# Loads of one image cut in eight parts, and a copy within DRAM cut in sixteen

## Chip, core and metric

The kernel runs on one core of a Trainium2 chip. The metric is the device time of one execution in microseconds (us), the median of three runs.

## What is computed

The input x has 4 images of 32 channels and 128 x 128 pixels. Layer 0 folds each 2 x 2 square of pixels into channels: 128 channels, 64 x 64 positions (cut from the reference):

```
xs = x.reshape(B, C, h, R, w, R).transpose(0, 1, 3, 5, 2, 4).reshape(B, C * R * R, h, w)
q = xs.reshape(B, C * R * R, hw)
energy = jnp.einsum('bci,bcj->bij', q, q)
d = jnp.sqrt(jnp.diagonal(energy, axis1=1, axis2=2))
attn = jax.nn.softmax(energy / (d[:, :, None] * d[:, None, :]), axis=-1)
out = gamma * jnp.einsum('bcj,bij->bci', q, attn) + xs      # and unfolded again
```

`energy` is 4096 x 4096 for each image, and symmetric. Layer 1 takes the result as tokens of 128 numbers, 4096 to an image: a linear attention with residual, then a mixture of eight experts of which each token uses two, with residual again.

## The kernel before

**Layer 0.** `attend` works on an image's 4096 positions in 8 chunks of 512. It goes through rows i = 0 to 7, and in row i through blocks (i, jc) with jc up to i, four steps to a block; step (i, t) is step t of row i, t = 4 jc + j. A step makes a 128 x 512 piece of the energy on TensorE (line 556, tile `pe`), its exponential on ScalarE (line 559, tile `pr`, "ACT" in the profile), and two steps later the product of it with q (line 440, tile `po`). Since the energy is symmetric, a block off the diagonal serves the other side too, transposed: VectorE (DVE) transposes pieces of 32 x 32 (line 369, tile `F`), and the rest of the transposition goes through DRAM. `move` writes `F` to a DRAM tile `blocks` (line 483), planned two steps after the block's last piece. `bring`, planned three steps later, reads it as tile `G` in four DMAs (line 491), and five steps later `transposed_share` starts to multiply it (line 375, tile `pg`), one quarter to a step. The diagonal blocks do the same with `below` (lines 498 and 506). So a block write has eight steps from its plan to its product, and a G load five. A full step has three pairs of products and takes 2.58 us.

**The loads of T.** Layer 1 needs the image's pixels again, by tokens. `input_rows` loads them into `T`, 32 rows of tokens in a partition, by `load_tokens` (line 279), which issues four DMAs on SP's queue for each call: four calls of eight rows, 128 KB to a DMA. The next image's first pixels are loaded by `prep` through the same function into `xx`.

**The copy within DRAM.** The experts' tokens are sorted through two DRAM tiles `xs`. Some of their places are never written, so `setup_sorting` fills both beforehand with any finite numbers: it copies pixels of x into them, eight DMAs of 624 KB on ACT's queue (line 154). The first scatter into `xs` starts at 514.9 us.

**The order.** PE, DVE, ACT and SP each run their instructions in the order in which the program issues them[...]. A table `timed` says when the side work goes in between the steps of image 0. An entry (generator, begin, end, count) lets the generator advance about `count` times between `begin` and `end` per cent of the image's clock; the clock goes up by 8 in a full step, by 4 more where a share goes along, and 1568 are an image. Two advances are made for each count, so a generator with two bare `yield`s after an item uses one count for it.

[...]

Of the kernel before, what the change touches and what calls it, by code (L numbers as in the profile page):

```python
# [22 lines left out]
def kernel(  # L23
# [43 lines left out]
    nc = tc.nc  # L67
    P = 128
    B, C, H, W = x.shape
# [6 lines left out]
    KT = 32  # L76
# [42 lines left out]
    NT = 2 * HR + E - 1  # L119
# [6 lines left out]
    xs = [dram.tile([NT * P, D], F32, tag=f"xs{h}", name=f"xs_{h}", bufs=1) for h in range(2)]  # L126
    xs_made, xs_read = ([], []), ([], [])
# [8 lines left out]
    def setup_sorting():  # L136
        def iota(dst, pattern, part=0):
            nc.gpsimd.iota(
                dst, pattern=pattern, base=0, channel_multiplier=part, allow_small_or_imprecise_dtypes=True
            )  # L140

        iota(rank_below, [[1, P]], part=-1)
        nc.vector.tensor_scalar(rank_below, rank_below, 0.0, None, ALU.is_gt)
        iota(upto, [[1, E], [-1, E]])
        nc.vector.tensor_scalar(upto, upto, 0.0, None, ALU.is_ge)
        iota(tiles_of[:, 0, :], [[P, HR]])
        iota(tile_no[:, :, 0], [[1, NT]])
        yield
        yield

        rows = x.rearrange("b c h w -> (b c h) w")
        step = NT * P // 4
        for g in range(8):
            inst = nc.scalar.dma_start(xs[g // 4][ts(g % 4, step), :], rows[ts(g, step), :])
            xs_made[g // 4].append(inst.ins)
            yield
            yield

# [19 lines left out]
    def idle(n):  # L178
        for _ in range(2 * n):
            yield  # L180
# [90 lines left out]
    def tokens(ap, b):  # L271
        return ap[b].rearrange("c (s k r) w -> s r c k w", s=2, r=2)

    def load_tokens(dst, b, k0, nk, queues=(nc.sync, nc.sync)):
        src = tokens(x, b)
        for s in range(2):
            for r1 in range(2):
                p0 = s * 64 + r1 * 32
                queues[r1].dma_start(dst[p0 : p0 + 32], src[s, r1, :, k0 : k0 + nk, :])
# [302 lines left out]
    def finish():  # L582

        while queued or late:
            yield
            tick[0] += 1
            turn_tick()
            clock[0] += 3 * NJ
            step_share()
            yield  # L590


    def input_rows(b, st):
        st["T"] = T = big1.tile([P, KT, D], F32, tag="T", name=f"T_{b}")
        for kc in range(4):
            load_tokens(T[:, ts(kc, 8), :], b, 8 * kc, 8)
            yield
            yield
            yield from idle(1)
# [703 lines left out]
    states = [{} for _ in range(B)]  # L1303
# [14 lines left out]
    timed = [(first, 0, 1, 4)]  # L1318
    for b in range(B):

        if b == 0:
            for kc, begin, end in ((1, 0, 5), (2, 6, 20), (3, 25, 45)):
                timed.append((prep(0, kc, states[0]), begin, end, 12))
            timed.append((setup_weights(), 46, 58, 9))
            timed.append((setup_sorting(), 58, 98, 9))
        if b + 1 < B:
            nxt = states[b + 1]
            timed.append((prep(b + 1, 0, nxt), 65, 82, 13))
            timed.append((prep(b + 1, 1, nxt), 83, 99, 13))
        timed.append((input_rows(b, states[b]), *((55, 75) if b in (0, B - 1) else (82, 99)), 9))  # L1330
        done = [0] * len(timed)
        start = clock[0]
        closing = None
        for half, _ in enumerate(chain(attend(b, states[b]), finish() if b == B - 1 else ())):
            if half % 2 == 0:
                t = 100 * (clock[0] - start) / UNITS
                moved = []
                if closing is None and t > 84:
                    closing = layer1(b, states[b])
                    steady.append([closing.first_parts() if b == B - 1 else closing.all_parts(), clock[0]])  # L1340
                for n, (steps, begin, end, count) in enumerate(timed):
                    if t >= begin and done[n] * (end - begin) < (t - begin) * count:
                        moved.append(steps)
                        done[n] += 1
                for stream in steady:
                    if clock[0] >= stream[1]:
                        stream[1] = clock[0] + PACE
                        moved.append(stream[0])
            for steps in moved:
                next(steps, None)  # L1350
        for steps, *_ in timed:
            for _ in steps:
                pass
        timed = []
        if b + 1 < B:
            timed.append((prep(b + 1, 2, nxt), 2, 20, 13))
            timed.append((prep(b + 1, 3, nxt), 30, 50, 13))
# [43 lines left out]
```

## Time and profile before

| | |
|---|---|
| median of three runs | 1744.91 us (1744.48 to 1747.42) |
| the profiled execution: its time, its span | 1753.19 us, 1751.4 us |
| mean granted TensorE clock | 0.983 |
| DMA, mean over the span | 204 GB/s |
| row 6 of image 0, from its first product to that of the diagonal | 207.65 to 281.92 us |
| T loads of image 0 on SP | from 213.45, 222.45, 251.01 and 267.03 us, four DMAs each |
| copies into `xs` on ACT | at 240.20, 255.72, 279.94, 295.24, 311.81, 325.99, 342.38, 358.55 us |

The profile is of one execution. A group names the line, the engine and the tiles (written <- read), the number of instructions, busy time and the mean of one, and then the time for which its engine stood idle just before them and what ended most of that. "SPq" and "ACTq" are DMA issues on those engines' queues. A wait is put down to the event that came last before it ended. In the order of time, a line has the start, the duration, the engine, the line of code and the tiles; brackets give the idle time before it and its releaser.

### The profile page before, as it was taken

What the parts mean: (1) busy time and instruction counts of PE and PEld (TensorE: products, weight loads), DVE (VectorE), ACT (ScalarE), POOL (GpSimd) and SP (SyncE); (2) the same over time, 40 slices, a digit from 0 to 9 for tenths busy, and PEclk for the clock granted to TensorE, in tenths of its full rate; (3) what the DMA queues carried; (4) which work ended last, traced back from release to release, by engine and by line L of the source; (5) the groups of instructions that cost most, each with busy time, mean ns of one, the idle gap of its engine ahead of it and who ended that gap; (6) DMA issues with size and microseconds to landing.
All of it is one profiled execution on the core that took longest, in us unless ns stands there. A gap on an engine that the chain in (4) does not pass through costs nothing. (4 is left out here: it accounts for less than half of the span.)

```text
span 1751.4 us, 21197 instructions
## 1 busy us (share of the span) xinstructions
PE 1667.8 (95%) x5458; PEld 882.2 (50%) x5458; DVE 939.7 (54%) x2443; ACT 927.0 (53%) x2893; POOL 512.0 (29%) x553
## 2 busy tenths in 40 slices
PE   8999998999999999899999999979999999899887
PEld 5444444455554455445554455535555455444633
DVE  4433333467485335566477334546748533455687
ACT  3555444466565555446565455536556455445376
POOL 1000000011026505540015622552102660463166
PEclk9999999999999999999999999989999999999989
DMA  4675877776568799997567799998656889995001
GB/s 136 195 207 166 217 200 222 237 212 190 165 195 239 232 276 252 264 243 197 164 189 223 227 273 264 251 244 224 192 166 196 251 223 271 265 267 133 1 13 37
DMA packets 240168, 355.24 MB, mean 203 GB/s; under 512 B 26928, under 2 KB 154928, under 8 KB 226096
## 3 DMA queue, kind: packets, MB, share of 16 engines
q1 hardware_dynamic: 219792, 314.91, 64.0%
q0 software_dynamic: 12288, 25.19, 5.1%
q10 hardware_dynamic: 7968, 13.77, 2.7%
q8 instruction: 46, 0.75, 0.2%
q14 instruction: 74, 0.61, 0.1%
HBM read 183.64 MB, written 173.15 MB: 204 GB/s over the span
## 5 line engine op out<-in xcount | busy, mean ns | idle before, releaser
L559 ACT ACTIVATE pr<-pe 128x512 f32<-128x512 f32 (+1 forms) x576 | 322.3, 560 | 546.3 <-PE pe L556 427.9
L440 PE MATMUL po<-pr,qT 128*128 128x512 f32 (+3 forms) x1152 | 553.2, 562 | 3.9 <-ACT o L445 3.5
L375 PE MATMUL pg<-G,qT 128*128 128x512 f32 x880 | 456.8, 601 | 37.5 <-DMA G<-blocks 25.6
L556 PE MATMUL pe<-qn,qn 128*128 128x512 f32 x896 | 464.7, 601 | 1.9 <-ACT pr L559 1.6
L369 DVE STREAM_TRANSPOSE F<-pr 128x512 f32<-128x512 f32 x440 | 305.9, 702 | 169.6 <-ACT pr L559 152.2
L440 PEld LDWEIGHTS po<-pr,qT 128*128 128x128 f32 x1152 | 217.1, 192 | 252.6 <-issue 224.8
L380 ACT ACTIVATE junk<-G 128x512 bf16<-128x512 f32 x440 | 273.1, 621 | 33.9 <-DMA G<-blocks 27.3
L375 PEld LDWEIGHTS pg<-G,qT 128*128 128x128 f32 x880 | 167.3, 192 | 239.6 <-issue 205.8
L1113 POOL DMA_INDIRECT yb<-ys,place x192 | 185.1, 964 | 275.6 <-DMA xn<-xs 103.2
L988 POOL DMA_INDIRECT xs<-xn,place x192 | 185.6, 967 | 125.5 <-issue 51.6
L556 PEld LDWEIGHTS pe<-qn,qn 128*128 128x128 f32 x896 | 156.0, 193 | 113.9 <-issue 103.5
L385 DVE TENSOR_TENSOR o<-o,pg 128x512 f32<-128x512 f32 x110 | 75.4, 685 | 201.4 <-PE pg L375 170.1
L164 POOL TENSOR_TENSOR rn<-ss,neg_half 128x8 f32<-128x8 f32 (+1 forms) x17 | 27.8, 1634 | 401.6 <-DVE ss L325 401.6
L559 ACT ACTIVATION_READ_ACCUMULATOR pr<-pe 128x1 f32 x576 | 112.1, 195 | 0.0
L1022 ACT ACTIVATE xn<-pys 128x256 f32<-128x256 f32 (+1 forms) x120 | 44.9, 376 | 116.1 <-PE pys L1055 69.3
L1048 PEld LDWEIGHTS pys<-ew_sb,xn 128*128 128x128 f32 x468 | 67.9, 191 | 57.2 <-issue 45.3
L164 POOL TENSOR_TENSOR rsf<-dm_f,neg_half 128x8 f32<-128x8 f32 (+1 forms) x15 | 26.2, 1746 | 235.1 <-DVE sv_f L635 235.1
L556 PE MATMUL pe<-qn 128*128 128x512 f32 (+3 forms) x256 | 90.2, 435 | 0.7 <-ACT qn L344 0.7
L380 ACT ACTIVATION_READ_ACCUMULATOR junk<-G 128x1 f32 x440 | 84.4, 192 | 0.0
L1048 PE MATMUL pys<-ew_sb,xn 128*128 x468 | 71.8, 276 | 11.4 <-ACT xn L1022 5.4
L1031 DVE COPY result<-pys 128x256 f32<-128x256 f32 (+1 forms) x60 | 24.6, 410 | 101.6 <-ACT xn L1022 46.2
L164 POOL TENSOR_TENSOR rsa<-dm_a,neg_half 128x8 f32<-128x8 f32 x16 | 26.4, 1647 | 167.4 <-DVE sv_a L635 167.1
(189 smaller groups left out, 1618.5 us busy)
## 6 DMA issues: line engine op xcount, KB each, us to landing
blocks<-F SPq DMA_DIRECT2D x108, 1024.0 KB
G<-blocks SPq DMA_DIRECT2D x432, 256.0 KB
xn<-xs SPq DMA_DIRECT2D x114, 128.0 KB
below<-F SPq DMA_DIRECT2D x31, 384.0 KB
G<-below SPq DMA_DIRECT2D x124, 96.0 KB
T<-in_x_dram SPq DMA_DIRECT2D x64, 128.0 KB
out_dram<-acc SPq DMA_DIRECT2D x128, 64.0 KB
xx<-in_x_dram SPq DMA_DIRECT2D x62, 128.0 KB
```

The costliest lines, as they stand in the source:

```text
L164: pinned(nc.gpsimd.tensor_tensor(dst, src, neg_half.to_broadcast(list(src.shape)), ALU.pow))
L369: f()
L375: nc.tensor.matmul(pg.rearrange("p (a f) -> p a f", a=4), st["qT"][i][:, ib, :], G[:, :, ib], start=(ib == 0), stop=(ib == NJ - 1),)
L380: nc.scalar.activation(junk, G[:, :, ib], AF.Copy, accum_out=st["sums"][:, NJ * i + ib, jc : jc + 1])
L385: nc.vector.tensor_tensor(o, o, pg.rearrange("p (a j c) -> p a j c", a=4, c=S), ALU.add)
L440: nc.tensor.matmul(row["po"][:, lo:hi], qT[blk // NJ][:, blk % NJ, :], w, start=start, stop=(row["left"] == 0))
L556: nc.tensor.matmul(pe[:, c0:], qn[jc][:, ts(j, P)], qn[i][:, c0:], start=True, stop=True)
L559: nc.scalar.activation(pr[:, c0:], pe[:, c0:], AF.Exp, accum_out=sums[:, t, i : i + 1]).ins
L988: inst = nc.gpsimd.indirect_dma_start(xs[h], offset(place[:, i, k : k + 1]), xn[:, k, :], None)
L1022: nc.scalar.activation(bufs[4 + g % 2][:, :n], p[:, : n * P].rearrange("p (j t) -> p j t", t=P), AF.Copy)
L1048: nc.tensor.matmul(p[:, 2 * P + j * D : 2 * P + j * D + D], bufs[4 + g % 2][:, j, :], weights[:, bass.ds(begins[2 * (g % 2) + j], D)], sta ...
L1113: inst = nc.gpsimd.indirect_dma_start(yb[k // 4][:, i, k % 4, :], None, ys, offset(place[:, i, k : k + 1]))
```

## The change

The copy into `xs` is made in sixteen DMAs of 312 KB in place of eight of 624 KB, with two `yield`s behind each as before. Image 0's T is loaded in eight calls of four rows (64 KB to a DMA) in place of four calls of eight; the other images keep four. In the table, the setup of the sorting gets a count of 17 between the same 58 and 98 per cent, and image 0's T goes from 55 to 75 per cent with a count of 9 to 52 to 94 per cent with 17. `idle(1)` is two more bare `yield`s.

```
-        step = NT * P // 4
-        for g in range(8):
-            inst = nc.scalar.dma_start(xs[g // 4][ts(g % 4, step), :], rows[ts(g, step), :])
-            xs_made[g // 4].append(inst.ins)
+        step = NT * P // 8
+        for g in range(16):
+            inst = nc.scalar.dma_start(xs[g // 8][ts(g % 8, step), :], rows[ts(g, step), :])
+            xs_made[g // 8].append(inst.ins)
             yield
             yield
@@
-        for kc in range(4):
-            load_tokens(T[:, ts(kc, 8), :], b, 8 * kc, 8)
+        nk = 4 if b == 0 else 8
+        for k in range(0, KT, nk):
+            load_tokens(T[:, k : k + nk, :], b, k, nk)
             yield
             yield
             yield from idle(1)
@@
-            timed.append((setup_sorting(), 58, 98, 9))
+            timed.append((setup_sorting(), 58, 98, 17))
@@
-        timed.append((input_rows(b, states[b]), *((55, 75) if b in (0, B - 1) else (82, 99)), 9))
+        begin, end, count = (52, 94, 17) if b == 0 else (55, 75, 9) if b == B - 1 else (82, 99, 9)
+        timed.append((input_rows(b, states[b]), begin, end, count))
```

## The prediction

> **What bounds the kernel now.** I read the page first, then the stretches of ten microseconds over image 0, then the waits of the SP queue, and last the order of time around the one hole that these showed.
>
> From the page: the costliest product that ever waits for a transfer, and the two transfers that the change cuts.
>
> ```profile
> PE 1667.8 (95%) x5458; PEld 882.2 (50%) x5458; DVE 939.7 (54%) x2443; ACT 927.0 (53%) x2893; POOL 512.0 (29%) x553
> L375 PE MATMUL pg<-G,qT 128*128 128x512 f32 x880 | 456.8, 601 | 37.5 <-DMA G<-blocks 25.6
> T<-in_x_dram SPq DMA_DIRECT2D x64, 128.0 KB
> xs<-in_x_dram ACTq DMA_DIRECT2D x8, 624.0 KB
> ```
>
> TensorE is busy 95% of the span, so a microsecond counts only where PE waits or runs slowly. The transposed products of line 375 waited 25.6 us for G tiles.
>
> The stretches (time, then busy us of PE, PEld, DVE, ACT, POOL, then TensorE's clock, DMA share, GB/s):
>
> ```profile
> 230.00:240.00 10.00, 10.00 (x26) 4.61 (x25) 3.15 (x5) 4.99 (x18) 0.00 (x0) 1.00 0.36 70
> 240.00:250.00 10.00, 10.00 (x27) 4.71 (x26) 4.02 (x6) 5.14 (x18) 0.00 (x0) 1.00 0.50 178
> 250.00:260.00 10.00, 8.59 (x20) 3.55 (x20) 2.73 (x4) 4.00 (x12) 0.00 (x0) 1.00 1.08 280
> 260.00:270.00 10.00, 6.23 (x15) 2.47 (x13) 2.73 (x4) 3.28 (x10) 0.00 (x0) 1.00 0.68 184
> 270.00:280.00 10.00, 7.74 (x15) 3.81 (x16) 1.40 (x2) 2.09 (x7) 0.00 (x0) 0.66 0.97 262
> ```
>
> Before PE's hole the DMA engines were almost idle (70 GB/s), and only afterwards full. So this is not lack of bandwidth: transfers were issued late. The waits of SP's queue in 225 to 250 us and 250 to 275 us name what held them, and the order of time shows it:
>
> ```profile
> SPq L483 <- DMA xs<-in_x_dram: 15.8, 1, 15.8
> SPq L279 <- DMA xs<-in_x_dram: 5.9, 1, 5.9
> ```
>
> ```profile
> 226.88 1.73 SPq L491 DMA_DIRECT2D G<-blocks  x4
> 244.51 0.34 SPq L483 DMA_DIRECT2D blocks<-F  x1
> 248.46 1.73 SPq L491 DMA_DIRECT2D G<-blocks  x4
> 254.79 9.80 SPq L279 DMA_DIRECT2D xx<-in_x_dram  x4
> 264.71 1.81 SPq L491 DMA_DIRECT2D G<-blocks  x4
> ```
>
> ```profile
> 240.20 0.59 ACTq L154 DMA_DIRECT2D xs<-in_x_dram  x1
> 255.70 1.10 PE L375 MATMUL pg<-G,qT 128*128 128x512 f32 x2 [1.41 <-DMA G<-blocks]
> 272.26 2.04 PE L375 MATMUL pg<-G,qT 128*128 128x512 f32 x2 [6.03 <-DMA G<-blocks]
> ```
>
> SP stood from 228.6 to 244.5 before a write of `blocks` whose data (the transposes of line 369) had been ready at 230.4. It shares no tile with `xs`; it waits because it stands eight places behind the first copy in the common order of DMAs, and that copy is ACT's, which reached it at 240.20. Then SP stood 5.9 us among the loads of xx, behind the second copy. The G tile of block (6,1) came 1.41 us late, that of (6,2) 6.03 us late. After the second hole two products took 2.04 us where they take 1.02. From 272.26 to 278.01 PE did work of 3.05 us (0.86 for each pair of products, 0.47 for four transposes): 2.7 us more. **The hole costs 1.41 + 6.03 + 2.7 = 10.1 us.** Nothing else in 205 to 440 us reaches a microsecond: 49.1 of 50, 29.8 of 30, 49.96 of 50, 79.2 of 80 us busy.
>
> [...] 4.3 us from the copy's issue to the write that it released, of which its data filled the DMA engines about 1.1 us (241.5 to 242.6). [...]
>
> **The change, part by part.**
>
> The same bytes move. T: 16 DMAs of 128 KB become 32 of 64 KB. SP issues one in 0.59 us (median of the 16 of before), so 16 more are about 9 us of SP's time over 40% of the image, from a queue that has been idle most of it; cost nothing while SP runs ahead. Copies: 8 more issues on ACT at 0.50 us are 4 us, one at a time. ACT is busy 5 of 10 us there and waits 1.28 us for PE in each step; PE takes an exponential two steps later. Nothing; without that cover 4 us. The DRAM copy in halves saves at most half of its 1.1 us of data; I take 4.0 us from issue to release in place of 4.3.
>
> What matters is the order. By the plan's arithmetic (clock units of 1568; 12 to a step of 0.77% where a share goes along) the copies of before fall at steps (6,12), (6,18), (6,24), (7,3) and so on, and T at (6,2), (6,8), (6,14), (6,20). After: copies at (6,9), (6,12), (6,16), (6,19), (6,22), (6,25), (7,1) and on, one in 3 steps; T at (5,21), (6,5), (6,11), (6,18), (6,25), (7,4), (7,11), (7,18). The xx loads stay at (6,16), (7,13).
>
> How long SP is held: in the common order SP's DMAs stand some 4 to 5 steps late against ACT (the first copy, of step (6,12), stands behind the first T load of (6,8)). So what stands eight places behind a copy of step x was planned at x - 4.5 plus the steps in which eight DMAs are planned. Before, with four T and four G loads planned in step (6,8), eight places were one step: the write of (6,9) waited for the copy of (6,12). That is 3 steps and the copy's 4.3 us: 3 x 2.58 + 4.3 = 12.0 us past its plan (seen: 244.51 - 233.08 = 11.4). The slack of a block write is 8 steps to its product, 20.6 us, less 4.0 us to its landing and 7.1 us from G's issue to the product that it released (248.46 to 255.70, rounded down): 9.5 us. Held 11.4 is 1.9 late; seen 1.41. So the measure works.
>
> After: 1.25 regular DMAs to a step, 0.62 of T, 0.33 copies are 2.2, and eight are 3.65 steps. What stands eight behind a copy was planned about at x - 0.85, and is held to x + 1.55: 2.4 steps, 6.2 us. A block write keeps 3.3 us of its 9.5. A G load has 5 steps less 7.1 us, 5.8 us of slack: 0.4 us late where one is hit. The dense place is (6,16), where xx and G(6,2) are planned together. If the copy of (6,19) stands ahead of all of these, the last piece of G(6,2) is held 4.55 steps, 11.7 us, and is 5.9 us late. If it stands inside the xx loads, block write (6,3) takes the wait, 3.55 steps or 9.2 us, within its slack. T is thinner there than before, which pulls SP forward in the order; I take the second as likelier.
>
> The sum: 10.1 us go. Bounds of what comes back: nothing, or 6 us with part of the slow clock, say 8. I take 2.2: five copies in row 6 that may each make one G load 0.4 us late. **Gain 8 us (between 2 and 10).** PE is the bound from there to the end of the image and the shift passes on: 24 more DMAs are three full rounds of eight, so later DMAs keep their semaphores. From the profiled run's own 1753.2 us (span 1751.4) to 1745.2; that run is 8.3 us over the median shown, so the median goes from 1744.9 to 1737. What is then latest in image 0 is the wait for the weights (PE 7.98 of 10 us in 180 to 190), which the change leaves.
>
> **The rivals.**
>
> *The wait is only moved.* Copy (6,19) or (6,22) takes the place of the first one and holds a G load 11.7 us. For it: the xx and T3 loads remain a cluster, with three copies beside them. Against: the two clusters of before are spread. Late by 6 us and part of the slow clock gives back 8: 1744.9 - 2 = 1743, no change.
>
> *Slower: sixteen ties in place of eight.* Each copy binds SP to ACT once, over the whole of rows 6 and 7. More DMAs could push SP's place in the order back to six steps. Then eight behind a copy is planned at x - 2.35, held 3.9 steps (10 us); a G load is 4.3 us late, a block write 0.6. With about six of 16 copies hitting a G load (4 G in 8 to 9 places, less those in which PE has already been shifted), at some 3 us each and the slow clock avoided, 18 us come in while 10 go: 1753. It decides from about five and a half steps of lag. For it: T and copies now reach to 97%. Against: the same bytes, and rows 6 and 7 of before, with and without T, stay at 4 to 5. [...]
>
> **How the numbers follow.** Likeliest 0.62, its own range 1733 to 1741; moved 0.19, 1741 to 1748; slower 0.19, 1748 to 1765. A measurement here tells 0.2% from no change, 3.5 us. Of the moved case a little is faster: faster 0.64, same 0.16, slower 0.20. The range 1733 to 1750 leaves out some 0.04 below and 0.14 above.
>
> **What would show it.** Right: no wait of SP on xs above 7 us in 225 to 275; PE above 9.5 of 10 us and clock 1.00 in each stretch from 250 to 280; G waits of line 375 down from 25.6 us to about 20. Wrong: a G wait of several us at row 6's later steps or in row 7 with a copy named in SP's waits; ACT waiting for a DMA at line 154; or PE whole in row 6 and the time unchanged, so that the gain was lost later.

## The result and the profile after

The changed kernel takes 1738.4 us, the kernel before 1745.0 us, medians of 20 runs each; the ratio is 0.9961, with a 95% interval of 0.9948 to 0.9973. That is 6.6 us less; 1737 was forecast, 8 us less. The profiled execution has a span of 1736.7 us.

The stretches of the changed kernel over the place of the old hole (columns as before):

```profile
230.00:240.00 10.00, 10.00 (x25) 4.53 (x24) 3.25 (x5) 4.99 (x17) 0.00 (x0) 1.00 0.84 239
240.00:250.00 10.00, 10.00 (x27) 4.69 (x27) 4.02 (x6) 5.24 (x18) 0.00 (x0) 1.00 0.65 161
250.00:260.00 10.00, 10.00 (x25) 4.50 (x24) 3.29 (x5) 5.18 (x16) 0.00 (x0) 1.00 0.79 254
260.00:270.00 10.00, 9.92 (x26) 4.38 (x25) 3.57 (x6) 4.22 (x14) 0.00 (x0) 1.00 0.91 265
270.00:280.00 10.00, 10.00 (x31) 5.26 (x30) 4.58 (x11) 5.38 (x19) 0.00 (x0) 1.00 0.81 254
```

From 250 us on PE is busy 9.92 to 10 of 10 us where it had 8.59, 6.23 and 7.74, and its clock stays at 1.00. The DMA engines, almost idle at 230 to 240 before (70 GB/s), move 239 there. SP's queue still waits for copies. Of its waits in 170 to 440 us, those for copies (us in total, number, longest), first before:

```profile
SPq L483 <- DMA xs<-in_x_dram: 20.9, 2, 15.8
SPq L279 <- DMA xs<-in_x_dram: 5.9, 1, 5.9
```

and in the changed kernel, where one more is of 0.3 us:

```profile
SPq L279 <- DMA xs<-in_x_dram: 10.1, 2, 5.7
SPq L483 <- DMA xs<-in_x_dram: 5.9, 1, 5.9
```

The waits have become shorter, and they hold other transfers. The order of time on SP's queue in the changed kernel shows which:

```profile
236.08 0.34 SPq L483 DMA_DIRECT2D blocks<-F  x1
236.46 7.23 SPq L279 DMA_DIRECT2D T<-in_x_dram  x4
243.88 1.91 SPq L491 DMA_DIRECT2D G<-blocks  x4
245.89 0.36 SPq L483 DMA_DIRECT2D blocks<-F  x1
246.30 8.82 SPq L279 DMA_DIRECT2D xx<-in_x_dram  x4
```

That these waits go by an order of DMAs, and not by tiles, is read from the two traces, which give with each DMA the number of the semaphore that tells of its landing. In the kernel before, SP's 99 DMAs from 205 to 380 us take eight numbers in turn and leave one out eight times; the numbers left out are, in the same sequence, those of ACT's eight copies. In the changed kernel they are 116 DMAs, and sixteen left out for sixteen copies. Taken together this is the prediction's common order. In the kernel before, the write of 244.51 us stands eight places behind the copy of 240.20 and has its number, and so has the last of the four xx loads (264.28) that of the copy of 255.72. From 228.6 to 244.51 us SP issued nothing; the DMAs behind the write came from 248.46 on.

The write of block (6,1) stood until 236.08 and not until 244.51, since the copy it waits for now comes at step (6,9), at 231.68 us, and not at (6,12). The next two waits fall on a T load and an xx load. But row 7 has two stalls that the kernel before does not have. The order of time on PE:

```profile
315.40 1.10 PE L375 MATMUL pg<-G,qT 128*128 128x512 f32 x2 [1.31 <-DMA G<-blocks]
339.47 1.10 PE L375 MATMUL pg<-G,qT 128*128 128x512 f32 x2 [2.29 <-DMA G<-blocks]
```

The best measure of all this is the length of rows 6 and 7: from one copy of the finished sums `po` (line 445) to the next. Two kernels were profiled twice, on different chips. Their row 6 agreed within 0.2 us and their row 7 within 0.7. This does not hold for every row: row 5 of the changed kernel took 67.8 and 65.8 us. The lengths below are of one execution for each kernel.

| kernel | row 6 of image 0, us | row 7, us |
|---|---|---|
| before | 81.07 | 83.64 |
| changed | 70.83 | 87.75 |
| changed, again on another chip | 70.98 | 87.11 |

So 10.2 us went in row 6 and 4.1 came back in row 7: 6.1 us, beside 6.6 in the medians. At the end of row 7 of image 0 the changed kernel is 6.0 us ahead. The two profiled executions are 14.7 us apart at their ends, but this cannot be put down to the change: the profiled run of before lies 8 us over its median, above all 20 of the runs compared here, and the medians are 6.6 us apart.

### The profile page after: what moved, and what is told of

Its sections match the earlier page's. It is cut to its first block, busy times and chain, and to the rows that moved or that the text cites. A ratio compares the mean times of both kernels' runs of the same rounds, so it can differ in the third digit from the quotient of the medians.

```text
span 1736.7 us, 21220 instructions
## 1 busy us (share of the span) xinstructions
PE 1660.1 (96%) x5458; PEld 879.4 (51%) x5458; DVE 940.4 (54%) x2443; ACT 928.7 (53%) x2893; POOL 513.3 (30%) x553
## 5 line engine op out<-in xcount | busy, mean ns | idle before, releaser
L375 PE MATMUL pg<-G,qT 128*128 128x512 f32 x880 | 455.5, 599 | 37.0 <-DMA G<-blocks 28.9
L1083 DVE SCALAR_TENSOR_TENSOR acc<-yb,weight,acc 128x128 f32<-128x128 f32 x192 | 65.6, 342 | 21.3 <-DMA yb<-ys,place 13.1
```

The source lines that it names most:

```text
L375: nc.tensor.matmul(pg.rearrange("p (a f) -> p a f", a=4), st["qT"][i][:, ib, :], G[:, :, ib], start=(ib == 0), stop=(ib == NJ - 1),)
L1083: nc.vector.scalar_tensor_tensor(a[:, k % 4, :], yb[k // 4][:, i, k % 4, :], weight[:, i, k, :], a[:, k % 4, :], ALU.mult, ALU.add)
```

## The experiments

The ratios are against the kernel before on the same chip, with 95% intervals. Three chips were used for the experiments, on which that kernel took 1745.0, 1759.6 and 1760.9 us. With "the tie" this part means that a DMA of SP waits, in the order that the two engines share, for one of ACT's copies, as the write did for 15.8 us in the kernel before. Where an edit adds lines, the code behind it stands one line further on (copies timed on GpSimd's queue) or two (pairs) than in the kernel before.

**T alone in eight parts** (the changed kernel with the old copy):

```
-        step = NT * P // 8
-        for g in range(16):
-            inst = nc.scalar.dma_start(xs[g // 8][ts(g % 8, step), :], rows[ts(g, step), :])
+        step = NT * P // 4
+        for g in range(8):
+            inst = nc.scalar.dma_start(xs[g // 4][ts(g % 4, step), :], rows[ts(g, step), :])
...
-            timed.append((setup_sorting(), 58, 98, 17))
+            timed.append((setup_sorting(), 58, 98, 9))
```

> Part of the change alone: T of image 0 in eight parts from 52 to 94 per cent, the copy still in eight DMAs of 624 KB at its old steps. Theory of order (an SP transfer stands in the common order eight places behind a copy that ACT reaches later; size does not matter): thinner T loads put more steps between, so the first stall (1.4 us) goes; the second copy, of step (6,18), still binds a piece of G(6,2), planned at (6,16): about 3.7 us late in place of 6.0. Row 6 ends (copy of its sums) at 287 to 290 us, where before it is 294.5 and after 284.4; row 7 loses some 3 to 4 us to T loads as the changed kernel does; total 0 to 4 us under before. Rival of size (the large copies fill the DMA engines and so delay G): the copies are as large as ever and the hole stays, row 6 ends at 292 to 295.

Measured: 0.9972 (0.9954 to 0.9991). Row 6 took 70.92 us, row 7 89.62. The hole went altogether, further than expected, with copies as large as ever. Row 7 lost 6.0 us, more than the 3 to 4 expected. On SP's queue:

```profile
230.75 0.38 SPq L483 DMA_DIRECT2D blocks<-F  x1
231.17 12.38 SPq L279 DMA_DIRECT2D T<-in_x_dram  x4
243.73 1.91 SPq L491 DMA_DIRECT2D G<-blocks  x4
```

The copy came at 239.06. SP waited for it 9.3 us, but in the middle of a T load, and the block write had passed at 230.75. Two more waits for copies, of 3.9 and 6.0 us, fall in row 7.

**The copies alone in sixteen** (the kernel before with the new copy and its count):

```
-        step = NT * P // 4
-        for g in range(8):
-            inst = nc.scalar.dma_start(xs[g // 4][ts(g % 4, step), :], rows[ts(g, step), :])
+        step = NT * P // 8
+        for g in range(16):
+            inst = nc.scalar.dma_start(xs[g // 8][ts(g % 8, step), :], rows[ts(g, step), :])
...
-            timed.append((setup_sorting(), 58, 98, 9))
+            timed.append((setup_sorting(), 58, 98, 17))
```

> The other part alone: sixteen copies of 312 KB, T in four parts from 55 to 75 per cent. Order: the copy of step (6,12) again stands eight places ahead of the block write of (6,1), and the one of (6,19) ahead of the last piece of G(6,2), held 4.5 steps; so the hole stays in spite of copies of half the size: row 6 ends at 292 to 297, SP waits on a copy for over 10 us in 225 to 250, the time is within 0.2% of before. Size: the hole goes, row 6 ends at 284 to 287 and the time is 7 to 10 us under before.

Measured: 0.9991 (0.9973 to 1.0009). Row 6 took 80.85 us, row 7 83.66. The hole stayed. Which transfers are held was not as expected: the first copy came at 229.65 and held a T load for 11.2 us, and the second held the write of (6,1) for 6.8:

```profile
221.46 12.97 SPq L279 DMA_DIRECT2D T<-in_x_dram  x4
234.59 1.75 SPq L491 DMA_DIRECT2D G<-blocks  x4
243.16 0.34 SPq L483 DMA_DIRECT2D blocks<-F  x1
```

PE's order of time has two stalls again:

```profile
256.97 1.10 PE L375 MATMUL pg<-G,qT 128*128 128x512 f32 x2 [3.98 <-DMA G<-blocks]
271.10 1.50 PE L375 MATMUL pg<-G,qT 128*128 128x512 f32 x2 [1.89 <-DMA G<-blocks]
```

**Copies of half the size, in pairs at the old steps** (before, with this in place of its copy; the two `yield`s behind it stay):

```
+        step = NT * P // 8
+        for g in range(16):
+            inst = nc.scalar.dma_start(xs[g // 8][ts(g % 8, step), :], rows[ts(g, step), :])
+            xs_made[g // 8].append(inst.ins)
+            if g % 2 == 0:
+                continue
```

> The kernel before with each copy cut in two of 312 KB, both issued at the old step. Order: the pair at (6,12) stands eight places ahead of a piece of G(6,0), planned at (6,8), and the pair at (6,18) ahead of xx loads; SP is held past (6,13), so the hole is as large as before or larger by some us: row 6 ends at 293 to 300. Size: half-size copies free the engines and the hole shrinks, row 6 ends below 290.

Measured: 0.9989 (0.9977 to 1.0001). Row 6 took 80.40 us and ended at 292.93, a little before the 293 to 300 expected from order; row 7 took 83.70. The wait (14.2 us) has moved to the G load of (6,0), as the order has it:

```profile
227.24 15.74 SPq L493 DMA_DIRECT2D G<-blocks  x4
243.08 0.38 SPq L485 DMA_DIRECT2D blocks<-F  x1
```

With these three the rival of size has fallen: halves don't remove the hole, and whole copies don't make it.

**The copies on GpSimd's queue**, first without more:

```
-            inst = nc.scalar.dma_start(xs[g // 4][ts(g % 4, step), :], rows[ts(g, step), :])
+            inst = nc.gpsimd.dma_start(xs[g // 4][ts(g % 4, step), :], rows[ts(g, step), :])
```

> The kernel before with one word changed: the eight copies of 624 KB are issued on GpSimd's queue, [...]so that no SP transfer waits for a copy. Bytes and sizes as before. Order: SP's waits on copies go, PE has no hole in 250 to 280, row 6 ends at 284 to 286, row 7 at 424 to 427 (no T loads there), time 9 to 11 us under before, a little under the changed kernel. Size: the large copies still fill the DMA engines, G is late by some us, row 6 ends at 290 to 295 and the time is that of before.

Measured: 0.9984 (0.9971 to 0.9996). Row 6 took 70.52 us and row 7 83.66, but this does not decide: GpSimd is not among the engines whose order the program fixes, and the copies were issued at 2.2 to 5.9 us, among the first loads of x. The first row ended 7.6 us late, and the gain of 9 to 11 us that was expected did not come. So the copies were tied to their steps:

```
+            inst = nc.gpsimd.dma_start(xs[g // 4][ts(g % 4, step), :], rows[ts(g, step), :])
+            wait_for(inst.ins, exps, "not before its step")
```

> The kernel before with its eight copies of 624 KB issued on GpSimd's queue, each made to wait for the exponential of its old step, so that they start where they started before, while no SP transfer waits for them any more. T in four parts as before. Order: nothing holds SP, row 6 (from the end of row 5 to its own end) takes 70.5 to 72 us in place of 81.1, row 7 83.7 as before, image 0 ends some 10 us earlier and the time is 8 to 10 us under before, 2 to 4 under the changed kernel. Size: copies of the old size at the old steps still delay G, row 6 takes 76 us or more.

Measured: **0.9940 (0.9918 to 0.9961), 1734.9 us**, the median of six runs, 10.1 us under before. Row 6 took 70.52 us, row 7 83.67. In order of time, GpSimd:

```profile
238.61 0.79 POOL L154 DMA_DIRECT2D xs<-in_x_dram  x1 [98.96 <-ACT pr L560]
252.99 0.52 POOL L154 DMA_DIRECT2D xs<-in_x_dram  x1 [13.59 <-ACT pr L560]
268.90 0.49 POOL L154 DMA_DIRECT2D xs<-in_x_dram  x1 [15.38 <-ACT pr L560]
```

The copies start at the old steps, with the old 624 KB, beside T in four old parts; and SP has no wait for a copy in 205 to 376 us. Its order of time:

```profile
228.99 0.34 SPq L484 DMA_DIRECT2D blocks<-F  x1
236.24 1.73 SPq L492 DMA_DIRECT2D G<-blocks  x4
240.33 0.34 SPq L484 DMA_DIRECT2D blocks<-F  x1
241.01 3.70 SPq L280 DMA_DIRECT2D T<-in_x_dram  x4
244.75 3.14 SPq L280 DMA_DIRECT2D xx<-in_x_dram  x4
```

The first of these is the write of (6,1), 228.99 in place of 244.51, and the xx loads take 3.14 us in place of 9.80. This is the cleanest test: the tie was taken, the bytes and the steps stayed, and the whole hole went. Three things changed along with it. ACT has lost eight issues of half a microsecond, the copies go through another DMA queue (in the trace of before, none of GpSimd's 384 DMAs has one of the eight numbers of SP and ACT), and the copies no longer stand among SP's DMAs, which presumably shifts the numbers of these (not shown). But the hole also went in both kernels that spread T and left the copies as they were on ACT's queue (above and below), so these three aren't needed for it to go. PE's stretches of 25 us:

```profile
225.00:250.00 25.00, 25.00 (x62) 11.46 (x61) 9.99 (x17) 12.97 (x42) 0.79 (x1) 1.00 0.93 253
250.00:275.00 25.00, 25.00 (x66) 11.76 (x65) 10.46 (x18) 12.29 (x40) 1.01 (x2) 1.00 0.94 262
```

**Spread or cut?** T in four parts, but over the new stretch (one line of before):

```
+        timed.append((input_rows(b, states[b]), *((52, 94) if b == 0 else (55, 75) if b == B - 1 else (82, 99)), 9))
```

> The kernel before with one line changed: T of image 0 still in four parts of 128 KB to a DMA, but over 52 to 94 per cent in place of 55 to 75 (steps (5,21), (6,10), (6,22), (7,9)); the copies as before. Order and spreading: four T DMAs fewer stand between a copy and the block write it held, row 6 takes 71 to 74 us; row 7 has one part of T in place of three and loses 0 to 2 us of the 4 to 6; 7 to 10 us under before. If it was the cutting of T into eight that mattered: row 6 takes 76 us or more.

Measured: 0.9959 (0.9943 to 0.9975). Row 6 took 70.53 us, row 7 86.74. So in row 6 the spreading did it, not the cutting. Row 7 lost 3.1 us with one part of T in it, more than the 0 to 2 expected; with the same copies and T in eight parts it lost 6.0.

**What row 7 loses.** The changed kernel with T's window moved, from (52, 94) to (50, 85) and to (54, 96):

> The changed kernel with T's eight parts from 50 to 85 per cent, so that two parts (steps (7,1), (7,7)) and not three fall in row 7, none just ahead of a block write, and none beside the xx loads of (7,13). T in row 7 as the cause of its loss: row 7 takes 83.7 to 85 us in place of 87.8. If row 7 lost through the sixteen copies: still 87 or more. Row 6, with parts closer together: 70.8 to 74.

> The changed kernel with T's parts two per cent later: the same three or four parts in row 7 ((7,0), (7,7), (7,14), (7,20)), but none just ahead of a block write. If the loss of row 7 comes from T's place directly ahead of the writes of (7,0) and (7,2): row 7 takes 84 to 85.5 us. If it is the load of the bytes on the queue: 87 or more as in the changed kernel. Row 6: 70.8 to 75.

Measured: 0.9959 (0.9949 to 0.9970) with row 6 at 72.38 and row 7 at 86.04 for the earlier window; 0.9990 (0.9979 to 1.0002) with 72.20 and 88.06 for the later. Neither window's row 7 came to what was expected if T's number there, or its place directly ahead of a block write, were the cause: 83.7 to 85 and 84 to 85.5. PE's order of time, earlier window and then later one:

```profile
337.85 1.10 PE L375 MATMUL pg<-G,qT 128*128 128x512 f32 x2 [2.14 <-DMA G<-blocks]
339.70 2.04 PE L375 MATMUL pg<-G,qT 128*128 128x512 f32 x2 [2.62 <-DMA G<-blocks]
```

T's place explains at most one of the two stalls. In neither window does a T load stand directly ahead of the write of (7,0), and in both the stall at 315 us is gone; the one near 339 us stays. The totals don't decide, since both windows also brought waits for copies into row 7 that the changed kernel does not have: 3.7 us at the G load of the diagonal in the earlier, 5.4 and 6.6 us at T loads in the later.

So T was put into row 7 without the tie: the changed kernel with eight copies on GpSimd, waiting for their steps, and then with the copies at the start:

> T as in the changed kernel (eight parts, 52 to 94 per cent) with the eight copies of 624 KB on GpSimd's queue at their old steps, so that no SP transfer waits for a copy. Asks where row 7's loss of 4.1 us comes from. If from T's own loads on SP's queue and the DMA engines: row 7 still takes 86 to 88 us, the time is 2 to 4 us over the same kernel with T from 55 to 75. If from waits of SP or ACT on copies by the common order: row 7 takes 83.7 to 84.5.

> The same, but without the wait for a step, so that the copies run at the very start of the kernel and rows 6 and 7 have none; this delays everything by some 7.6 us. If row 7's loss needs the copies' bytes beside T's: row 7 takes 83.7 to 84.5 us. If T alone makes it: 86 to 88.

Measured: 0.9948 (0.9932 to 0.9964), row 6 70.52, row 7 **83.64**, for the first; 1760.3 us in one run for the second, where the first row ends 8.3 us late, and row 7 83.65. T in row 7 costs nothing when SP is not bound to ACT's copies. The bytes don't make the loss either, since the first of these kernels moves both T and the copies in row 7. So the loss needs the tie. Whether it needs T in row 7 as well is not isolated: before, the copies alone and the pairs have the tie, no T in row 7 and no loss (83.64, 83.66, 83.70), but all three had the hole in row 6, in which PE fell behind together with SP. How tie and T can meet is read on SP's queue. Without the tie (first of these two kernels, order of time):

```profile
229.62 0.38 SPq L484 DMA_DIRECT2D blocks<-F  x1
291.02 1.73 SPq L507 DMA_DIRECT2D G<-below  x4
292.80 3.19 SPq L280 DMA_DIRECT2D T<-in_x_dram  x4
296.09 0.38 SPq L484 DMA_DIRECT2D blocks<-F  x1
300.31 1.86 SPq L492 DMA_DIRECT2D G<-blocks  x4
```

and in the changed kernel:

```profile
297.69 1.98 SPq L506 DMA_DIRECT2D G<-below  x4
299.72 3.48 SPq L279 DMA_DIRECT2D T<-in_x_dram  x4
303.29 0.38 SPq L483 DMA_DIRECT2D blocks<-F  x1
307.61 3.17 SPq L491 DMA_DIRECT2D G<-blocks  x4
```

Counted from the end of row 5 (211.47 and 213.56), the write of (6,1) stands at 18.2 and 22.5 us, the G load of the diagonal at 79.6 and 84.1, the write of (7,0) at 84.6 and 89.7. The changed kernel's SP is 4 to 5 us late from its first wait for a copy, and carries this to row 7, though no wait for a copy over 0.3 us is seen after 255 us. In row 7 T loads take up to 3.7 us each of the time in which it could catch up. In the kernel before, without them:

```profile
305.78 2.85 SPq L506 DMA_DIRECT2D G<-below  x4
308.73 0.38 SPq L483 DMA_DIRECT2D blocks<-F  x1
```

Counted from the end of row 6, the write of (7,0) comes 14.2 us later there, 14.1 without the tie, and 18.9 in the changed kernel; the G load of the diagonal, ahead of any T load of row 7, comes 11.3, 9.0 and 13.3 us later. In the changed kernel's row 7 (285 to 372 us) SP's longest waits are those until its own block writes have landed, time that it cannot make up:

```profile
SPq L491 <- DMA blocks<-F: 36.8, 7, 6.6
```

That a late SP finds too little free time in row 7, and that T takes part of it, is argued from these times. That the loss goes with the tie is shown.

**The two side by side**, each kernel again in one set of runs:

> The changed kernel again, beside the next one on the same chip: 0.3 to 0.5% under before.

> The kernel before with its copies on GpSimd's queue at their old steps, again: 0.5 to 0.7% under before and 0.1 to 0.3% under the changed kernel.

Measured: 0.9971 (0.9956 to 0.9985) for the changed kernel and 0.9937 (0.9918 to 0.9955) for the kernel before with timed copies on GpSimd: 1755.1 and 1749.2 us where before takes 1760.9. The second beats both kernels, by 0.6% and 0.3%.

## Why the prediction was right

- *The hole is a wait in the order of DMAs, not bandwidth, and costs 10.1 us.* Shown: without the tie row 6 is 10.6 us shorter, with the same copies at the same steps; the change itself took 10.2 off it.
- *What stands eight behind a copy is held some 6.2 us.* The holds came, but fewer and shorter. Only the first three copies held SP for more than 0.3 us, where five in row 6 had been allowed for. SP stood for 5.9, 4.4 (10.1 less 5.7) and 5.7 us. The 6.2 us were counted from the step for which the transfer was planned. Counted so, as in the prediction's 11.4 us for before, the write of (6,1) was held 2.9 us: its step (6,9) starts at 233.18 on PE. PE did not wait for its G tile.
- *Later DMAs keep their semaphores.* They did: SP's last 1031 DMAs, from 354.5 us on in the changed kernel and from 359.9 before, have the same numbers in both traces.
- *The copy of (6,19) stands inside the xx loads or ahead of them.* It did neither. The copy that held an xx load, until 254.8 us, is the one before it, of step (6,16), issued at 248.43. The copy of (6,19) came at 256.15, when SP had issued all of these. What the prediction drew from this came true all the same: no G load made PE wait in row 6 for more than 0.2 us.
- *"I take 2.2: five copies in row 6 that may each make one G load 0.4 us late."* This term was wrong in its place and its size. Row 6 gave back at most 0.3 us (70.83 beside 70.52 without the tie); row 7 gave back 4.1, in a kernel whose SP comes to it late. The prediction had costed T's loads at nothing "while SP runs ahead", and did not ask whether SP still runs ahead in row 7. With 4.1 in place of 2.2, the sum is 6.0 us. It is luck that 2.2 us, allowed for something that did not happen, made up for part of this; without them the forecast would have been 10 us less.
- *The copy's part.* I treated both parts as one spreading of the order. The runs separate them: T's spread brings the whole of the 10.2 us in row 6 (70.92 without the new copies), the sixteen copies alone nothing (80.85). With them row 7's loss is 4.1 us and not 6.0; the times of the whole kernel, 0.9961 and 0.9972, do not tell the two apart.
- *Signs.* No wait on xs above 7 us: so it was. PE above 9.5 of 10 and clock 1.00 in 250 to 280: so it was. G waits of line 375 down from 25.6 us to about 20: this did not come. Over the whole run they went to 28.9, while up to 450 us they went from 9.5 to 5.7. The sum over four images was a bad sign for a change in the first. One sign of being wrong came in part: PE was whole in row 6, and four of the ten microseconds were lost again later.
- *Slower: sixteen ties in place of eight.* It did not come, and the sixteen ties alone made no difference that the runs could tell (0.9991).
- *The copy's 4.3 us.* The prediction reads 1.1 us of data in them. This reading is wrong, as the last section shows; nothing in the sum rests on it beyond 0.3 us.

## What to carry to other kernels

Where a queue waits for a transfer with which it shares no tile, look for an order that two engines share: here SP stood 15.8 us for a copy of ACT's, and cutting the copies in two did not help (0.9991 and 0.9989). Give such side transfers a queue of their own, tied to the step at which they should start; here that one word and one wait gained 0.6%, and spreading the loads 0.3 to 0.4%. And a queue that "runs ahead" has a lead that can be used up: ask, stretch by stretch, what still stands in front of it.

## What the runs showed of the hardware that was not expected

A stretch of the profile counts a DMA packet where it starts, with all of its duration, so that its DMA share can be above 1. A copy within DRAM can then look shorter than it is. The stretch in which the first copy of before has its data:

```profile
241.50:242.60 1.10, 1.10 (x4) 0.44 (x3) 0.69 (x2) 0.64 (x2) 0.00 (x0) 1.00 1.93 581
```

A DMA share of 1.93 over 1.10 us is 2.1 us of work for each engine. In the packets themselves, data begin 1.4 us after the issue and end at 3.9; the release follows at 4.25. So its data took 2.5 of the 4.25 us, the larger part. The first copy of 312 KB, issued at 231.68, took 4.3 us as well, but in other parts: its data took 1.4 us in place of 2.5, and began 2.4 us after the issue and not 1.4, in a stretch in which the DMA engines were busy (239 GB/s beside 70). From issue to release the copies that held SP took 4.3, 8.6 and 6.8 us with 624 KB, and 4.3, 3.1 and 6.4 us with 312 KB. How much halving saves is not shown by so few.

In these runs the length of a wait alone does not tell whether PE's clock falls. In the kernel before, the clock was 1.00 in 250 to 260 us, in which a wait of 1.41 us ended, and 0.66 in 270 to 280, in which the one of 6.03 ended. It was halved at once after a wait of 2.62 us (T's later window: products of 2.04 us at 339.70 in place of 1.02, clock 0.57 in 340 to 343). With the copies alone it was halved about 1 us after a wait of 3.98 us (1.10 us at 256.97, then 1.80; clock 0.80 in 255 to 260), and again within the first products after one of 1.89 us (1.50 us at 271.10; clock 0.67 in 270 to 275). It stayed at 1.00 from 240 to 255 us with the pairs, where PE stood for 3.25 us in 240 to 250. What decides it is not shown.
